# Single-value copies of VectorE moved ahead of the third block's statistics at the layer change of a two-layer graph network

## The chip, the core and the metric

The kernel runs on one core of a Trainium2 chip. Five engines work side by side, each through its own list of instructions in order: TensorE multiplies matrices (the profile shows it as PE, and its weight loads as PEld), VectorE (DVE), ScalarE (ACT) and GpSimd (POOL) do the element-wise work, and SyncE (SP) issues DMA transfers. Instructions of different engines meet only at semaphores: an instruction waits until a counter of another engine has reached a number. TensorE writes its results to PSUM[...], from which VectorE and ScalarE read.

The metric is the device time of one execution in microseconds, the median of three runs. All figures below in us are from such runs or from one profiled execution.

## The reference, cut to what matters

There are 8 batch elements `x[b]` of 2048 tokens and 256 features, and one adjacency matrix of 2048 x 2048. Layer 0 is an attention with four heads whose softmax runs over chunks of 256 keys, with output projection, residual and two normalisations. Layer 1 is a graph attention:

```python
h = relu(layernorm(x))                       # layer 1: statistics over the 256 features
h = h @ W                                    # 2048 x 256
e_src, e_dst = h @ a1, h @ a2                # one value per token each
e = where(adj == 0, -1e9, leaky_relu(e_src[:, None] + e_dst[None, :], 0.01))
x = x + relu(softmax(e) @ h)
```

The kernel keeps `W` with two further columns, `W a1` and `W a2`, in `w1s` (128 x 2 x 258), so that one matrix product gives `h` (256 columns) and the two values per token (columns 256 and 257) at once.

## The kernel before

**Tiling.** A batch element is cut into four blocks of 512 tokens, called `zero`, `low`, `mid` and `last` (class `Between`), and a block into four tiles of 128 tokens (`TB = 4`). Between the attention of one batch element and the products of its graph attention lies a stretch of some 45 us, the layer change, written out by hand from `if ahead:` on (line 1260). `ahead` is the projection of the next batch element: its matrix products are laced into the layer change of the present one. There are 8 batch elements; the first 7 take the branch `if ahead`, the last one the `else` branch, which the change does not touch.

**Order.** The kernel runs under a manual schedule: on every engine the instructions stand in the order in which the Python calls make them. A wait at the head of an engine's list therefore holds everything behind it on that engine.

**The steps that meet here**, in the order of the calls before the change:

- `mid.stats1([t])` (`Between.stats1`, which calls `norm_stats`, lines 356 and 357): `bn_stats` and `bn_aggr` of VectorE over tile `t` of the third block's `x4`. Tiles 2 and 3 of that block are finished by a GpSimd addition, `x<-x,o` at line 792 (`mid.add(1)`), which stands in GpSimd's list behind the issue of the last `ctxT<-prod` transfer (line 578, `gather`).
- `low.values(t, bank)` (line 843): two matrix products of 128 x 258 into a PSUM tile. Tiles 0 and 1 go to `ps_s` buffers, tiles 2 and 3 to `ps_t` buffers.
- `low.keep(t)`: ScalarE copies 256 columns to `g` (line 851), then VectorE copies the two last columns to `sd` (line 852, 128 x 2, two single values per token). Only when both are done can TensorE write to that PSUM buffer again.
- `low.sum1()` (line 838, ScalarE), `zero.fetch1()` (line 155, a DMA).
- `mid.power1()`, `mid.shift1()`, `mid.norm1(0)`, `mid.norm1(1)`: ScalarE (lines 361 to 363), VectorE (line 367, `rn`), ScalarE (line 379). They need the statistics of all four tiles.
- `ahead.values(0)` (line 461): eight matrix products of 128 x 256 into a `ps_n` buffer, then eight into a `ps_t` buffer; VectorE adds a bias and moves each to `v` (line 466).
- `ahead.qk(1, 0, halves=[0])` (line 447): four products of 128 x 512 into a `ps_n` buffer.
- `last.output(0)`, `last.output(1)` (line 721): eight products each from `ctxT`, which the transfer of line 578 completes; into a `ps_t` and a `ps_n` buffer. VectorE takes them up at line 757.

**PSUM.** The tags `s`, `n` and `t` have two buffers each. In this stretch `ps_m()` hands out `ps_n` and `ps_t` by turns. So the first `ps_t` of `ahead.values(0)` is the buffer that held `low.values(2)`, and the `ps_t` of `last.output(0)` the one that held `low.values(3)`. In the built program the first product of `ahead.values(0)` on `ps_t` waits for VectorE's count up to the copy of tile 2, and that of `last.output(0)` for the count up to the copy of tile 3.

**What waits for what on ScalarE.** In the built program each copy of line 852 waits for the ScalarE copy of line 851 of its own tile; both read the same PSUM buffer.

Of the kernel before, what the change touches and what calls it, by code (L numbers as in the profile page):

```python
# [28 lines left out]
def gnn_two_layers(  # L29
# [26 lines left out]
    TB = NB // P  # L56
# [335 lines left out]
    class Projection:  # L392
# [40 lines left out]
        def fetch(self, nb):  # L433
            self.hT[nb] = Features(turned_d[0][nb])
# [47 lines left out]
    class Attention:  # L482
# [100 lines left out]
        def early(self, part):  # L583

            if part == 0:
                for kt in range(KT):
                    self.logits(0, 0, kt)
                    self.logits(0, 1, kt)
            elif part == 1:
                for o in range(2):  # L590
                    self.clip(0, o)
                    self.exponentials(0, o)
                for kt in range(KT):
                    self.logits(0, 2, kt)
                    self.logits(0, 3, kt)
            elif part == 2:
                self.clip(0, 2)
                self.exponentials(0, 2)
                self.clip(0, 3)
                self.add(0, 0)  # L600
            if part == 3:
                for kt in range(KT):
                    self.logits(1, 0, kt)
# [305 lines left out]
    class Layer1:  # L909
# [56 lines left out]
        def weights(self, nb, j4, tiles=range(4), w=None):  # L966
            if w is None:
                w = work.tile([P, 4, NB], F32, tag="e", name="w", bufs=5)
            for i in tiles:
                j = 4 * j4 + i  # L970
                nc.vector.tensor_scalar(  # L971
                    w[:, i, :], self.src[nb], self.cd[:, 0, j:j + 1], self.cd[:, 1, j:j + 1],
                    op0=ALU.mult, op1=ALU.max,
                )
                if i % 2:
                    two = w[:, i - 1:i + 1, :]
                    nc.vector.scalar_tensor_tensor(  # L977
                        two, bounds1[nb, j // 8][:, j % 8 - 1:j % 8 + 1, :], 0.0, two, op0=ALU.is_gt, op1=ALU.mult
                    )
            return w  # L980
# [186 lines left out]
    for b in range(B):  # L1167
# [3 lines left out]
        zero, low, mid, last = blocks  # L1171
# [87 lines left out]
            block.adder = nc.vector  # L1259
        if ahead:  # L1260
            for t in range(TB):
                mid.stats1([t])
                low.values(t, ps_h if t < 2 else ps_t)
                low.keep(t)
            low.sum1()
            zero.fetch1()
            mid.power1()
            mid.shift1()
            mid.norm1(0)
            mid.norm1(1)  # L1270
            ahead.values(0)
            ahead.fetch(2)
            ahead.qk(1, 0, halves=[0])
            last.output(0)
            last.output(1)
            mid.flip1(0, "both")
            last.take(0)
            mid.flip1(1)
            last.take(1)
            mid.send1()  # L1280
            one.send(1)
            zero.sum1()
            last.stats(range(TB))
            ahead.qk(1, 0, halves=[1])
            last.power()
            last.shift()
            last.scaled(range(TB))
            ahead.qk(1, 1)
            for t2 in range(2):
                last.gamma(t2)  # L1290
                last.add(t2)
            for t in range(TB):
                last.stats1([t])
                zero.values(t)
                zero.keep(t)
            one.send(0)
            mid.fetch1()
            last.power1()
            last.shift1()
            last.norm1(0)  # L1300
            last.norm1(1)
            ahead.values(1)
            ahead.qk(2, 0)
            last.flip1(0, "both")
            last.flip1(1)
            last.send1()
            ahead.fetch(3)
            mid.sum1()
            ahead.qk(2, 1)
            mid.ends(1)  # L1310
            last.fetch1()
            one.receive(0)
            ahead.values(2)
            one.targets(0, 3 * TB)
            one.received(0)
            one.receive(1)
            ahead.qk(3, 0)
            weights(0)
            ahead.qk(3, 1)
            last.sum1()  # L1320
            last.ends(1)
            one.total()
            one.targets(3 * TB, NT)
            weights(1)
            one.send(2)
            one.send(3)
            ahead.values(3)
        else:
            one.weights(0, 0, range(2, 4), ws[0])
            low.ends(1, [ps_t, ps_t, ps_n, ps_n])  # L1330
            low.sum1()
            one.send(1)
            mid.stats1(range(TB))
            mid.power1()
            mid.shift1()
            accs[0] = one.accumulators(0)
            early(0)
            mid.norm1(0)
            mid.norm1(1)
            one.targets(TB, 2 * TB)  # L1340
            one.receive(1)
            last.output(0)
            last.output(1)
            weights(1)
            last.take(0)
            last.take(1)
            mid.ends(0)
            last.stats(range(TB))
            for t in range(TB):
                if t == 2:  # L1350
                    last.power()
                    last.shift()
                mid.values(t)
                mid.keep(t)
            one.targets(2 * TB, 3 * TB)
            weights(2)
            fetch(11)
            last.scaled(range(TB))
            one.received(1)
            for t2 in range(2):  # L1360
                last.gamma(t2)
                last.add(t2)
            early(1)
            last.stats1(range(TB))
            last.power1()
            last.shift1()
            weights(3)
            last.norm1(0)
            last.norm1(1)
            early(2)  # L1370
            last.ends(0)
            one.total()
            last.ends(1)
            one.mean()
            one.targets(3 * TB, NT)
            weights(4)
            fetch(12)
            one.send(2)
            one.send(3)
            one.receive(2)  # L1380
            one.alone(0)
# [81 lines left out]
```

## Time and profile before

| | us |
|---|---|
| median of 3 runs | 3513.77 |
| lowest and highest run | 3513.32, 3514.57 |
| profiled execution, its own time | 3513.01 |
| span of the profiled execution (first to last instruction) | 3511.2 |
| DVE busy | 2630.4 (75%) |
| ACT busy | 1959.2 (56%) |
| POOL busy | 1825.5 (52%) |
| mean granted TensorE clock | 1.000 |

The span is 1.8 us shorter than the time of the same execution; that rest lies before the first and after the last instruction of the program. The seven layer changes of the branch `if ahead` begin at 347.81, 781.25, 1214.26, 1647.28, 2080.35, 2513.36 and 2946.38 us (the first product of line 843 on `ps_s`), so a batch element takes about 433.0 us. The granted clock is full throughout, so no stretch has to be corrected for it.

In the rows of a timeline the first number is the start in us from the beginning of the span, the second the duration from the first start to the last end of the row's instructions, then follow engine, line, operation, `out<-in`, shapes and the number of instructions. In brackets stands how long the engine idled before the row and who ended that. A row of `x8` is eight instructions that follow each other.

### The profile page before, as it was taken

What the parts mean: (1) busy time and instruction counts of PE and PEld (TensorE: products, weight loads), DVE (VectorE), ACT (ScalarE), POOL (GpSimd) and SP (SyncE); (2) the same over time, 40 slices, a digit from 0 to 9 for tenths busy, and PEclk for the clock granted to TensorE, in tenths of its full rate; (3) what the DMA queues carried; (4) which work ended last, traced back from release to release, by engine and by line L of the source; (5) the groups of instructions that cost most, each with busy time, mean ns of one, the idle gap of its engine ahead of it and who ended that gap; (6) DMA issues with size and microseconds to landing.
All of it is one profiled execution on the core that took longest, in us unless ns stands there. A gap on an engine that the chain in (4) does not pass through costs nothing.

```text
span 3511.2 us, 104599 instructions
## 1 busy us (share of the span) xinstructions
PE 3498.5 (100%) x46076; PEld 2300.0 (66%) x46076; DVE 2630.4 (75%) x3983; ACT 1959.2 (56%) x2961; POOL 1825.5 (52%) x1198
## 2 busy tenths in 40 slices
PE   9999999999999999999999999999999999999999
PEld 5455775667765577566876758656686655864568
DVE  7887677877678676786767867678686785857876
ACT  6777426763267633676336763367623776147751
POOL 5687017870278702786037850378503784047841
PEclk9999999999999999999999999999999999999999
DMA  7545323443234431444324443244432335224331
GB/s 246 129 108 123 94 87 73 97 113 102 68 87 86 118 100 61 92 93 109 102 61 92 92 105 102 66 91 87 119 105 64 79 85 125 63 55 92 80 78 53
DMA packets 171320, 332.13 MB, mean 95 GB/s; under 512 B 28656, under 2 KB 90352, under 8 KB 170864
## 3 DMA queue, kind: packets, MB, share of 16 engines
q1 hardware_dynamic: 129712, 205.36, 18.6%
q0 software_dynamic: 32832, 119.03, 18.5%
q8 instruction: 360, 5.90, 0.7%
q10 hardware_dynamic: 8320, 1.05, 0.2%
q14 instruction: 96, 0.79, 0.1%
HBM read 156.50 MB, written 51.44 MB: 59 GB/s over the span
## 4 chain that ended last, share of the span: by engine, by line
PE 97%; DVE 1%; ACT 1%; POOL 1%; issue 0%; DMA 0%; ACTq 0%; DVEq 0%; POOLq 0%
PE ps_s L503 25%; PE ps_n L519 25%; PE ps_s L994 12%; PE ps_t L531 6%; PE ps_n L994 6%; PE ps_t L994 6%; PE ps_t L743 2%; PE ps_t L447 2%; PE ps_n L447 2%; PE ps_s L447 2%; PE ps_t L461 2%; PE ps_n L461 1%; PE ps_n L843 1%; PE ps_t L843 1%; PE ps_z L296 0%
## 5 line engine op out<-in xcount | busy, mean ns | idle before, releaser
L543 DVE SCALAR_TENSOR_TENSOR e<-ps_s,bound 128x1024 f32<-128x1024 f32 x1024 | 1219.3, 1221 | 401.3 <-PE ps_s L503 396.4
L558 POOL TENSOR_TENSOR both<-e 128x1024 f32<-128x1024 f32 x512 | 1222.4, 2418 | 541.8 <-PE ps_t L531 244.6
L503 PE MATMUL ps_s<-q,k 64*32 64x512 f32 x16384 | 1335.2, 590 | 0.1
L552 ACT ACTIVATE e<-e 128x1024 f32<-128x1024 f32 x1024 | 1049.3, 1049 | 456.2 <-DVE e L543 438.8
L519 PE MATMUL ps_n<-e,v 64*32 64x512 f32 x16384 | 1121.2, 589 | 0.0
L503 PEld LDWEIGHTS ps_s<-q,k 64*32 64x32 f32 x16384 | 505.2, 106 | 403.3 <-issue 277.9
L519 PEld LDWEIGHTS ps_n<-e,v 64*32 64x32 f32 x16384 | 522.0, 107 | 366.3 <-issue 266.5
L531 PE MATMUL ps_t<-both,ones 64*32 64x512 f32 x4096 | 548.7, 590 | 0.0
L994 PE MATMUL ps_s<-g,w 128*128 128x257 f32 x2048 | 448.5, 380 | 0.0
L994 PEld LDWEIGHTS ps_s<-g,w 128*128 128x128 f32 x2048 | 388.4, 190 | 56.0
L573 DVE TENSOR_TENSOR prod<-ps_n,rz 128x512 f32<-128x512 f32 x448 | 288.7, 687 | 135.0 <-ACT rz L564 86.5
L1017 POOL TENSOR_TENSOR x<-x,r 128x256 f32<-128x256 f32 x124 | 90.7, 745 | 457.8 <-ACT r L1015 457.0
L977 DVE SCALAR_TENSOR_TENSOR w<-bound,w 128x1024 f32<-128x1024 int8 x256 | 314.7, 1229 | 8.7
L367 POOL TENSOR_TENSOR krn<-krn,mv 128x4 f32<-128x4 f32 x28 | 6.8, 243 | 566.1 <-DVE w L971 566.1
L994 PE MATMUL ps_n<-g,w 128*128 128x257 f32 x1024 | 292.4, 382 | 0.0
L994 PE MATMUL ps_t<-g,w 128*128 128x257 f32 x1024 | 289.7, 380 | 0.0
L563 ACT ACTIVATE rz<-ps_t 128x512 f32<-128x512 f32 x256 | 152.6, 596 | 237.3 <-PE ps_t L531 164.2
L971 DVE TENSOR_SCALAR w<-src,cd 128x512 f32<-128x512 f32 x512 | 263.2, 556 | 18.1 <-ACT src L951 14.2
L994 PEld LDWEIGHTS ps_n<-g,w 128*128 128x128 f32 x1024 | 192.8, 190 | 44.3 <-issue 17.6
L578 POOL DMA_DIRECT2D ctxT<-prod x224 | 192.3, 858 | 56.5 <-DVE prod L573 49.5
L531 PEld LDWEIGHTS ps_t<-both,ones 64*32 64x32 f32 x4096 | 152.3, 105 | 100.7 <-SPq L475 45.1
L994 PEld LDWEIGHTS ps_t<-g,w 128*128 128x128 f32 x1024 | 193.8, 189 | 28.2
(139 smaller groups left out, 2975.2 us busy)
## 6 DMA issues: line engine op xcount, KB each, us to landing
ctxT<-prod POOLq DMA_DIRECT2D x224, 512.0 KB, 5.0
bound<-bound_d SPq DMA_DIRECT2D x125, 512.0 KB, 4.7
turned_d<-squares SPq DMA_DIRECT2D x232, 128.0 KB, 2.9
hT<-turned_d SPq DMA_DIRECT2D x58, 512.0 KB, 4.5
rows<-in_adj_dram SPq DMA_DIRECT2D x32, 512.0 KB, 5.3
x<-in_x_dram SPq DMA_DIRECT2D x32, 512.0 KB, 6.3
out_dram<-x SPq DMA_DIRECT2D x31, 512.0 KB, 2.6
xp<-in_x_dram SPq DMA_DIRECT2D x28, 512.0 KB, 4.4
```

Source lines behind the costliest of these rows:

```text
L447: nc.tensor.matmul(in_key_order(pp) if i == 0 else pp, w[:, di, do * P:(do + 1) * P], h, start=di == 0, stop=di == FC - 1,)
L503: nc.tensor.matmul(self.s[n, o][c * Q:(c + 1) * Q, kt, :], self.k[p][rows, at:at + Q], self.q[p][rows, nb * NB:(nb + 1) * NB], start=True, ...
L519: made.append(nc.tensor.matmul(self.num[n, c][h * Q:(h + 1) * Q, :], self.v[rows, j * KT + kt, at:at + Q], self.e[n, p][rows, i * KT + kt, :],
L531: nc.tensor.matmul(self.total[n][h * Q:(h + 1) * Q, :], ones[rows, :], self.both[n, h // 2][rows, h % 2, :], start=half == 1, stop=half == 0,)
L543: nc.vector.scalar_tensor_tensor(self.e[n, p][:, i * KT:(i + 1) * KT, :], self.s.pop((n, o)), -CLIP * SC, bounds[nb, j // 4][:, j % 4 * KT ...
L552: nc.scalar.activation(e, e, AF.Exp, scale=1.0 / SC)
L558: nc.gpsimd.tensor_tensor(self.both[n, p], e[:, 0], e[:, 1], op=ALU.add)
L573: nc.vector.tensor_tensor(dst[:, c, :], self.num.pop((n, c)), self.rz[n], op=ALU.mult)
L578: nc.gpsimd.dma_start(self.ctxT[nb], self.prod.pop(n), accum_op=ALU.add)
L971: nc.vector.tensor_scalar(w[:, i, :], self.src[nb], self.cd[:, 0, j:j + 1], self.cd[:, 1, j:j + 1], op0=ALU.mult, op1=ALU.max,)
L977: nc.vector.scalar_tensor_tensor(two, bounds1[nb, j // 8][:, j % 8 - 1:j % 8 + 1, :], 0.0, two, op0=ALU.is_gt, op1=ALU.mult)
L994: nc.tensor.matmul(accs[t][:, 0:F + 1], w[:, i, t * P:(t + 1) * P], g[:, j, :], start=j == 0, stop=j == NT - 1,)
```

## The change

In the first lines of the branch `if ahead` the order of the calls is altered. Nothing is added or removed; the number of instructions on each engine is the same.

```diff
         if ahead:
             for t in range(TB):
-                mid.stats1([t])
                 low.values(t, ps_h if t < 2 else ps_t)
                 low.keep(t)
+                if t:
+                    mid.stats1([t - 1])
+            mid.stats1([TB - 1])
             low.sum1()
```

`low.values` issues only to TensorE and `low.keep` to ScalarE and VectorE, `mid.stats1` only to VectorE. So the lists of TensorE, ScalarE, GpSimd and SyncE stay as they are, instruction for instruction. VectorE's list changes in seven places, one in each layer change with a next batch element:

```
before: stats 0, copy 0, stats 1, copy 1, stats 2, copy 2, stats 3, copy 3
after:  copy 0, copy 1, stats 0, copy 2, stats 1, copy 3, stats 2, stats 3
```

Here "stats t" stands for the two instructions of lines 356 and 357, and "copy t" for the one of line 852. In the built program the waits follow: the `ps_t` product of `ahead.values(0)` waits for a VectorE count that is lower by four (copy 2 stands two tiles' statistics nearer the front), the first product of `last.output(0)` again for the count of copy 3, and ScalarE's line 361 for the count of the last aggregation in place of that of copy 3.

## The prediction, made before the changed kernel ran

> **What bounds the kernel now.** I read the page's first and fourth parts first: which engine is never idle, and which one the end hangs on.
>
> ```profile
> PE 3498.5 (100%) x46076; PEld 2300.0 (66%) x46076; DVE 2630.4 (75%) x3983; ACT 1959.2 (56%) x2961; POOL 1825.5 (52%) x1198
> PE 97%; DVE 1%; ACT 1%; POOL 1%; issue 0%; DMA 0%; ACTq 0%; DVEq 0%; POOLq 0%
> ```
>
> TensorE is idle for 3511.2 - 3498.5 = 12.7 us and carries 97% of the chain of waits. What the other engines do counts only where it makes TensorE wait, so the second view is the list of who waited for the copies of line 852:
>
> ```profile
>   PEld ps_t L461: 7.1, 7
>   PE ps_t L461: 4.3, 7
> ```
>
> TensorE stood still seven times in front of the second half of `ahead.values(0)`, until a copy of two values per partition was done: one stall for each layer change that has a next batch element. The third view is the timeline there, TensorE first, in the third of the seven:
>
> ```profile
> 1216.11 1.91 PE L843 MATMUL ps_t<-w1s,hT 128*128 128x258 f32 x8
> 1217.86 1.89 PE L461 MATMUL ps_n<-wvT,hT 128*128 128x256 f32 x8
> 1220.30 1.99 PE L461 MATMUL ps_t<-wvT,hT 128*128 128x256 f32 x8 [0.55 <-DVE sd L852]
> 1222.13 1.88 PE L447 MATMUL ps_n<-hT,wqT 128*128 128x512 f32 x4
> 1223.85 1.89 PE L721 MATMUL ps_t<-woT,ctxT 128*128 128x256 f32 x8
> 1225.57 1.89 PE L721 MATMUL ps_n<-woT,ctxT 128*128 128x256 f32 x8
> ```
>
> Then VectorE, and the GpSimd rows that it waits for:
>
> ```profile
> 1217.52 0.13 DVE L852 COPY sd<-ps_s 128x2 f32<-128x2 f32 x1
> 1217.57 0.42 DVE L356 BATCH_NORM_STATS2 stats<-x 128x6 f32<-128x256 f32 x1
> ...
> 1219.55 0.43 DVE L356 BATCH_NORM_STATS2 stats<-x 128x6 f32<-128x256 f32 x1 [1.31 <-POOL x L792]
> 1220.02 0.18 DVE L357 BATCH_NORM_AGGREGATE mv<-stats 128x2 f32<-128x6 f32 x1
> 1220.12 0.13 DVE L852 COPY sd<-ps_t 128x2 f32<-128x2 f32 x1
> ```
>
> ```profile
> 1217.35 0.86 POOL L578 DMA_DIRECT2D ctxT<-prod  x1 [7.19 <-DVE prod L573]
> 1217.96 1.56 POOL L792 TENSOR_TENSOR x<-x,o 128x512 f32<-128x512 f32 x1
> ```
>
> The copy of tile 2 is not late by itself: it stands behind the statistics of tile 2, and these wait 1.31 us for GpSimd's addition, which ends at 1219.52. A short copy is held by a wait that it does not need, and TensorE is held by the copy (done 1220.25, product at 1220.30).
>
> **What the stall costs.** The page's idle time is measured against modelled ends, so I take starts. Eight products of 128x256 occupy 1225.57 - 1223.85 = 1.72 us when nothing is in the way; from the `ps_n` half to the `ps_t` half it is 1220.30 - 1217.86 = 2.44, 0.72 too much. The stalled half itself takes 1222.13 - 1220.30 = 1.83, another 0.10 too much (its row is 1.99 long against 1.89): the pipe has to fill again. Together 0.82 us. In the first layer change the halves start at 351.41 and 354.27 and the next row at 356.10: 2.86 - 1.73 + 0.10 = 1.23, since GpSimd's issue of the transfer, and so its addition, comes 0.42 later there (start 3.52 us after the first product of line 843, against 3.09). The other five are like the third: of the 4.3 us in the list above 0.97 is the first one's, and 6 x 0.55 = 3.3 the rest; VectorE's waits for that addition, 9.6 us in seven times, are in the same way 1.73 + 6 x 1.31. Sum: 1.23 + 6 x 0.82 = **6.15 us**.
>
> Rule against row: the Trainium skill, "Perfetto Trace Analysis", section "Identifying the Most-Contended Engine", says that busy time of the matmuls is no good measure of how near TensorE is to its limit, because they are pipelined, and that the busy share of the weight loads is to be used. For this sum the matmul rows would give 4.3 us of idle time, the weight loads 7.1. The starts decide between them: 4.3 leaves out the tail that the model adds to the last product, 7.1 takes in a pause that a weight load has before an undisturbed product too. 4.3 and 7.1 are the two ends that I keep for the range.
>
> **The change part by part.**
>
> *Copies 0 and 1 in front of statistics 0.* Two instructions of 0.13 to 0.16 us. Their ScalarE copies ended at 1216.01 and 1216.70, before VectorE is through with `prod` (1217.06), so they start at once. They delay statistics 0 and 1 by about 0.1 us each; nobody reads these before statistics 3 is done. Cost 0; the cover is VectorE's idle 1.31 us.
>
> *Copy 2 in front of statistics 1.* Two copies, one pair of statistics and the copy after 1217.06: 0.06 + 0.06 + 0.42 + 0.14 + 0.13, so done by about 1217.8, where the undisturbed `ps_t` half is due at 1217.86 + 1.72 = 1219.58. Margin 1.8 us: the stall goes whole. The rows of VectorE overlap (the copy at 1217.52 runs to 1217.65, the statistics start at 1217.57), so a copy holds the next operation up by some 0.05; at its full 0.16 it would be 1218.0, and the margin would hold too.
>
> *Copy 3 in front of statistics 2.* It has to wait for ScalarE's copy of tile 3. "PSUM — Partial Sum Buffer", section "PSUM bank collisions raise a hardware error", asks that two engines be kept apart on one bank even where both read, and the program does have VectorE wait for ScalarE. The rule speaks against putting such copies ahead of work that needs no ScalarE. The row:
>
> ```profile
> 1218.05 0.38 ACT L851 ACTIVATE g<-ps_t 128x256 f32<-128x256 f32 x1 [0.49 <-PE ps_t L843]
> ```
>
> It ends at 1218.43. VectorE reaches copy 3 at about 1218.3, waits 0.15 and is done at 1218.6, still 0.9 us before GpSimd frees statistics 2. By the rule up to 0.2 us of VectorE's time, by the rows none on the path: 0.
>
> *Statistics 2 and 3 without copies between them.* The last aggregation ends at about 1220.75, where copy 3 ended at 1220.84. ScalarE's line 361 waits for that, so `power1`, `shift1` and `norm1` come 0.08 earlier. Nothing for TensorE.
>
> **What is late next.** TensorE reaches line 447 at 1221.3 and `last.output(0)` at 1223.03 (first layer change: 356.58). That needs `ctxT`: issued at 1217.35, landed 4.7 us later by the DMA view of this window, 1222.1 (first: 351.33 + 4.8 = 356.1). Margins 0.9 and 0.4: no new wait. `last.output(1)`, due at 1224.75, needs the `ps_n` buffer that line 466 empties; VectorE is through with that at 1222.5, behind line 367. Margin 2.2. All that follows (line 757, the last block's statistics, the transfers of its and `mid`'s turned tiles) hangs on these products and moves up with them. From 1260 to 1647 the view of stretches shows TensorE busy for all of 140.00 and 247.00 us, so there is no later wait that could eat the gain. A second small hole, 7 x 0.17 us before `ahead.values(1)` (line 461 on `ps_n`, 2.2 us of the weight loads' waits for line 852), is at the end of such a chain and stays as it is.
>
> **Sum.** The profiled execution took 3513.01; minus 6.15 gives 3506.9. The median of the runs shown is 0.76 higher, so I forecast **3507.6**. A difference of less than 0.2%, 7.03 us, can't be told from no change here; the forecast lies inside it by 0.9 us.
>
> **The rivals.**
> - *More than the stall goes* (0.13). If the 7.1 us of the weight loads are the truer measure, or the small second hole closes too (6.15 + 1.2 = 7.35), the time is 3506.4 to 3506.7, faster by just over the bound. For: both numbers stand in the profile. Against: the chain into the second hole moves up with TensorE, so the hole should stay.
> - *The transfer takes the stall's place* (0.08). The margin before `last.output(0)` is 0.4 to 0.9 us, and over the whole program this transfer lands after 4.5 to 7.8 us. Landing 1.3 us later than now would give back 0.4 to 0.9 in each, some 3 us: 3510.6; more than 1.8 us later gives back all: 3513.8. Against: the transfer's issue and its neighbours are unchanged, and in the two layer changes that I read it took 4.7 and 4.8.
> - *The stall doesn't go* (0.04): another wait sits under the same product. Then 3513.8. The built order lists only VectorE's count there.
> - *ScalarE holds the copies, and these the statistics* (0.05): the slower side. Copy 3 now stands ahead of statistics 2 and 3 and waits for ScalarE. If it came later than 1219.5, the whole row statistics, lines 361 to 367, line 466 would be late. Its end must leave 3.0 us for that row before 1224.75, so it decides from about 1221.7 on; to cost 7 us beyond the gain, (6.15 + 7.0)/7 = 1.9 us more each, ScalarE's copy would have to end at 1223.6 and not at 1218.43. Time 3520.8. Its list is unchanged, hence the small chance.
>
> **How the numbers follow.** The forecast has 0.70: 3506.8 to 3508.4 with the spread of the runs (1.25 us from lowest to highest). The range, 3506.3 to 3510.6, takes in the first rival and half of the second. Faster by over 0.2%: 0.13 and the lower tail of the forecast, together 0.20. Slower: 0.06. Within: 0.74.
>
> **What would show it.** Right: the waits for line 852 no longer name `PE ps_t L461`; its `ps_t` half starts 1.72 us after its `ps_n` half; the sixteen products' rows are both 1.89 long; VectorE's idle time before statistics 2 is still ended by GpSimd; from one layer change to the next it is 432.2 us, not 433.0. Wrong: a new idle time in brackets before line 721 or 843, above all one ended by a DMA or by ScalarE, or an unchanged 433.0.

## The result, and the profile after

| | before | after |
|---|---|---|
| median of 22 runs, us | 3513.81 | 3507.69 |
| span of the profiled execution, us | 3511.2 | 3506.3 |
| start of the first layer change, us | 347.81 | 349.03 |
| from one layer change to the next, us | 433.44, then 433.01 to 433.07 | 432.19 to 432.27 |

The change saves 6.12 us: the ratio is 0.9983, with an interval from 0.9977 to 0.9989, that is 3.9 to 8.1 us. The saving is 0.17%, inside the 0.2% within which the forecast counted a difference as none, and yet clear of no change with this many runs. Three single runs far above the rest (20027.53 us before, 8030.45 and 4592.26 after) are not in the ratio; without them the medians are 3513.80 and 3507.67. The spans differ by 4.9 only because the set-up of this one execution, before the first layer change, took 1.2 us longer; counted from there to the end, 3163.4 us became 3157.3, 6.1 less.

The first part of the page, and from the view of who waited for the copies of line 852 the group of those that waited:

```profile
PE 3496.3 (100%) x46076; PEld 2309.8 (66%) x46076; DVE 2630.3 (75%) x3983; ACT 1958.5 (56%) x2961; POOL 1824.3 (52%) x1198
```

```profile
who waited for it (us, times):
  POOL ctxT L578: 50.2, 7
  ACT rn L361: 8.7, 8
  ACT cd L933: 3.6, 16
  PEld ps_n L461: 2.2, 7
  PEld ps_s L843: 0.2, 1
```

The two rows for `ps_t L461`, 4.3 and 7.1 us, are gone; `ps_n L461` with 2.2 is still there. (That GpSimd's `ctxT` stands in the list is no new wait: the transfer goes out 3.09 us into the layer change as before. The view names the last count of VectorE before that, now a copy's.) TensorE's timeline in the third layer change, which begins at 1213.42:

```profile
1217.01 1.89 PE L461 MATMUL ps_n<-wvT,hT 128*128 128x256 f32 x8
1218.73 1.89 PE L461 MATMUL ps_t<-wvT,hT 128*128 128x256 f32 x8
1220.46 1.88 PE L447 MATMUL ps_n<-hT,wqT 128*128 128x512 f32 x4
1222.18 1.89 PE L721 MATMUL ps_t<-woT,ctxT 128*128 128x256 f32 x8
```

Each row starts 1.72 or 1.73 us after the one above, no idle time stands in brackets, and both rows of line 461 are 1.89 long: neither the stall nor the filling of the pipe is left. VectorE beside it:

```profile
1216.12 0.22 DVE L852 COPY sd<-ps_s 128x2 f32<-128x2 f32 x2
...
1216.81 0.13 DVE L852 COPY sd<-ps_t 128x2 f32<-128x2 f32 x1
...
1217.62 0.16 DVE L852 COPY sd<-ps_t 128x2 f32<-128x2 f32 x1
1218.70 0.43 DVE L356 BATCH_NORM_STATS2 stats<-x 128x6 f32<-128x256 f32 x1 [0.92 <-POOL x L792]
```

Statistics 2 still wait for GpSimd's addition, and start at the same moment as before, 5.28 us into the layer change (5.29 before); only no copy stands behind them any more.

### The profile page after: what moved, and what is told of

Same layout as the page of the kernel before. It is cut to its first block, busy times and chain, and to the rows that moved or that the text cites. A ratio compares the mean times of both kernels' runs of the same rounds, so it can differ in the third digit from the quotient of the medians.

```text
span 3506.3 us, 104599 instructions
## 1 busy us (share of the span) xinstructions
PE 3496.3 (100%) x46076; PEld 2309.8 (66%) x46076; DVE 2630.3 (75%) x3983; ACT 1958.5 (56%) x2961; POOL 1824.3 (52%) x1198
## 4 chain that ended last, share of the span: by engine, by line
PE 98%; DVE 1%; DMA 1%; ACT 0%; POOL 0%; issue 0%; ACTq 0%; DVEq 0%; POOLq 0%
PE ps_s L503 25%; PE ps_n L519 25%; PE ps_s L994 12%; PE ps_t L531 6%; PE ps_n L994 6%; PE ps_t L994 6%; PE ps_t L743 2%; PE ps_t L447 2%; PE ps_n L447 2%; PE ps_s L447 2%; PE ps_n L461 2%; PE ps_t L843 1%; PE ps_t L461 1%; PE ps_n L843 1%; PE ps_s L843 0%; DMA bound_d<-bound_part 0%
```

## The experiments

All times are medians of 6 to 21 runs, to be held against 3513.8 to 3514.0 for the kernel before in the same sessions and 3507.69 for the changed one. The 95% interval of each ratio is 0.0013 to 0.0025 wide, 5 us and more, so differences of some 1 us are read from the profiled execution instead: from the start of the first layer change to the end, where the kernel before takes 3163.4 us and the changed one 3157.3.

### Which copy carries the gain

Of the kernel before, copy 2 alone is moved, ahead of statistics 2:

```diff
-                mid.stats1([t])
+                if t != 2:
+                    mid.stats1([t])
                 low.values(t, ps_h if t < 2 else ps_t)
                 low.keep(t)
+                if t == 2:
+                    mid.stats1([t])
```

> The kernel before with one copy moved: VectorE's copy of tile 2 ahead of statistics 2, copies 0, 1 and 3 where they were. My theory (copy 2 alone holds TensorE, by standing behind statistics 2 that wait for GpSimd): the whole gain, 6.15 us, 3507.7, and the ps_t half of line 461 starts 1.72 us after the ps_n half. Rival (all the copies in front, or the shorter row of statistics, bring the gain): at most a part of it, 3510 or more.

Measured: 3507.64 us, ratio 0.9982 (0.9974 to 0.9989). One exchanged pair brings the whole gain (3157.3 us from the first layer change to the end, as in the changed kernel). The counterpart has copies 0 and 1 in front and leaves 2 and 3 behind their statistics:

```diff
-                mid.stats1([t])
+                if t == 2:
+                    for u in range(3):
+                        mid.stats1([u])
+                if t == 3:
+                    mid.stats1([t])
```

> The kernel before with copies 0 and 1 in front, but copy 2 behind statistics 2 and copy 3 behind statistics 3 as before. My theory: no gain, 3513.8, and the stall of 0.72 us before the ps_t half stays, 0.97 idle in the first layer change and 0.55 in the others. Rival (any relief of VectorE's list ahead of the statistics helps): a part of the 6.15 us, 3508 to 3512.

Measured: 3513.81 us, ratio 1.0 (0.9992 to 1.0008). TensorE's timeline there (its third layer change begins at 1215.01):

```profile
1218.60 1.89 PE L461 MATMUL ps_n<-wvT,hT 128*128 128x256 f32 x8
1221.04 1.99 PE L461 MATMUL ps_t<-wvT,hT 128*128 128x256 f32 x8 [0.55 <-DVE sd L852]
```

It is the stall of before to the hundredth: 2.44 from start to start, 0.55 idle, and from the first layer change to the end it takes 3163.4 us as before. Two of the four copies moved without any effect.

### Is it the copy's place, or GpSimd's lateness

VectorE's list as before; GpSimd's addition goes half an attention step earlier:

```diff
-            at(18 if soon else 20, lambda: self.add(1))
+            at(18 if soon else 19 if self.nb == NNB - 2 else 20, lambda: self.add(1))
```

> The kernel before, VectorE's list untouched; GpSimd's addition (line 792, second half of the third block) is issued half an attention step earlier, ahead of the last ctxT transfer in GpSimd's list. My theory: statistics 2 no longer wait, copy 2 is done about 1.0 us before TensorE wants the buffer, and the whole 6.15 us are gained without moving a copy: 3507.7. Rival (VectorE's own work ahead of copy 2, eight instructions, is what is too long): the stall shrinks only in part, 3510 to 3513.

Measured: 3508.12 us, ratio 0.9984 (0.9977 to 0.9991). VectorE's timeline, third layer change from 1214.64:

```profile
1218.54 0.42 DVE L356 BATCH_NORM_STATS2 stats<-x 128x6 f32<-128x256 f32 x1
1219.00 0.18 DVE L357 BATCH_NORM_AGGREGATE mv<-stats 128x2 f32<-128x6 f32 x1
1219.10 0.13 DVE L852 COPY sd<-ps_t 128x2 f32<-128x2 f32 x1
```

With the addition done in time the statistics do not wait, and copy 2, still behind three pairs of them, is done at 1219.23, when TensorE wants the buffer only at 1214.64 + 5.32 = 1219.96. So the stall needs both: a copy behind the statistics, and statistics that wait for GpSimd. To remove either is enough. The 0.4 us that this version stays behind is visible in the trace (3157.8 against 3157.3): line 757 now waits for GpSimd too, which takes one more semaphore instruction, so it starts 12.48 and not 12.41 us into the layer change, and the products behind the second hole start 0.07 later, seven times.

### What the slower side would have taken

All four copies in front, so that VectorE waits for ScalarE with none of the statistics done:

```diff
-                mid.stats1([t])
                 low.values(t, ps_h if t < 2 else ps_t)
                 low.keep(t)
+            for t in range(TB):
+                mid.stats1([t])
```

> All four copies ahead of all four statistics. VectorE then waits for ScalarE's copy of tile 3 (ends 4.17 us after the first product of line 843) with nothing done of the statistics; the last aggregation ends some 0.2 us later than in the changed kernel (6.6 against 6.46). My theory: that is inside the margin, 3507.7. Rival (a wait for ScalarE put in front of the statistics is passed on to TensorE): 0.2 us in each of seven layer changes, 3509.1, or more if the normalisation is late for line 466.

Measured: 3508.00 us, ratio 0.9983 (0.9976 to 0.999). The two expectations lie 1.4 us apart and the runs of one kernel spread by more (3507.24 to 3509.85), so the time alone leans to the first without deciding. TensorE's starts decide for the first: they are those of the changed kernel to 0.01 us in the whole third layer change. To find where the margin ends, work for nobody is put between statistics 2 and 3 of the changed kernel:

```diff
+            spare = small.tile([P, TB, 2], F32, tag="spare", name="spare", bufs=2)
+            norm_stats(mid.x4, spare, [0] * 3)      # 8 in the second kernel
             mid.stats1([TB - 1])
```

> The changed kernel with three more pairs of statistics (tile 0 again, into a tile that nobody reads) on VectorE between statistics 2 and 3: some 3 x 0.53 = 1.6 us more before lines 361, 367, 379 and 466. My theory (the row of statistics has a margin of 2.2 us before it empties the ps_n buffer that the second half of line 721 needs): no loss, 3507.7, at most 3508.5 where the two transposes come close to line 757. Rival (work on VectorE in this stretch is passed on to TensorE): 7 x 1.6 = 11 us, 3519.

> The same with eight more pairs, some 4.2 us. My theory: the margin is used up, the second half of line 721 starts about 2.0 us late, 0.1 for filling the pipe again, and up to 0.5 more at the next hole, line 461 of the second block: 7 x 2.6 = 18 us, 3526. Rival (passed on in full): 7 x 4.2 = 30, 3537. Rival (all hidden): 3507.7.

Measured: 3507.37 and 3524.39 us, ratios 0.9981 (0.9973 to 0.999) and 1.003 (1.0018 to 1.0042). 1.6 us of additional work seven times cost nothing; 4.2 us cost (3524.39 - 3507.69)/7 = 2.4 each, so what is passed on begins between the two. Where it comes out, from the list of TensorE's waits and its timeline (third layer change from 1217.31), both with eight more pairs:

```profile
PE ps_n L721 <- DVE v L466: 12.3, 7, 2.1
```

```profile
1226.07 1.89 PE L721 MATMUL ps_t<-woT,ctxT 128*128 128x256 f32 x8
1229.65 1.99 PE L721 MATMUL ps_n<-woT,ctxT 128*128 128x256 f32 x8 [1.69 <-DVE v L466]
```

It is the place that the prediction named, the `ps_n` buffer of line 466. The second half starts 3.58 us after the first instead of 1.72, 1.86 late; with the pipe to fill and the next holes a little wider that makes the 2.4. 2.6 was expected. Line 466 starts 3.95 us later than in the changed kernel and 1.86 of this is passed on, so its margin is 2.1 us, where the prediction had 2.2.

### The second hole

The same exchange where the statistics of the last block and the copies of the first block's values alternate:

```diff
-                last.stats1([t])
                 zero.values(t)
                 zero.keep(t)
+                if t:
+                    last.stats1([t - 1])
+            last.stats1([TB - 1])
```

> The changed kernel, and the same reordering at the second such place, where the statistics of the last block and the copies of the first block's values alternate. There TensorE stands 0.07 us and fills its pipe for 0.10 before line 461 on ps_n, seven times 0.17. My theory: the copies have nothing to wait for, so the hole closes: 1.2 us, 3506.5. Rival (the hole is of another cause, or moves to the next product): 3507.7.

Measured: 3506.44 us, ratio to before 0.9979 (0.997 to 0.9988). The two timelines, first the changed kernel, then this one:

```profile
1233.40 1.03 PE L843 MATMUL ps_t<-w1s,hT 128*128 128x258 f32 x4
1234.35 1.99 PE L461 MATMUL ps_n<-wvT,hT 128*128 128x256 f32 x8
```

```profile
1232.51 1.03 PE L843 MATMUL ps_t<-w1s,hT 128*128 128x258 f32 x4
1233.38 1.89 PE L461 MATMUL ps_n<-wvT,hT 128*128 128x256 f32 x8
```

0.95 from start to start has become 0.87, and the row is 0.10 shorter: 0.18 x 7 = 1.26 us, and 3507.69 - 3506.44 = 1.25 are measured (1.3 in the trace, 3156.0 against 3157.3). This version is faster than both kernels.

### The transfer's margin

The prediction gave line 721 a margin of 0.4 to 0.9 us over the landing of `ctxT`. To use it up, the issue is held back in GpSimd's list until copy 3 is done (GpSimd's addition of line 792, no longer behind it, is then over before the layer change begins):

```diff
+            after_copies = small.tile([P, 1], F32, tag="held", name="held", bufs=2)
+            nc.gpsimd.tensor_copy(after_copies, sd[:, 0, 2 * TB - 1:2 * TB])
+            att.gather(STEPS - 1)       # no longer issued within the attention
             zero.fetch1()
```

> The changed kernel, the issue of the last ctxT transfer held in GpSimd's list until VectorE's copy 3 is done (a one-element copy of GpSimd in front of it waits for that): issued some 1.5 us later, at about 4.6 us after the first product of line 843, landing at about 9.4, where line 721 is due at 8.76. My theory of the transfer's margin (0.9 us, 0.4 in the first layer change): line 721 stands 0.6 to 0.75 us and fills its pipe for 0.1, the gain is about given back, 3512.5 to 3513.5. Rival (ample cover, or line 721 waits for something later than the transfer already): 3507.7.

Measured: 3525.20 us, ratio 1.0033 (1.002 to 1.0045). Both expectations failed: 17.5 us were lost and not 5 to 6. From the list of TensorE's waits, from its timeline and from the DMA view of the third layer change (there the last figure is from issue to landing), the late transfer; line 723 is line 721 of the other kernels:

```profile
PE ps_t L723 <- DMA ctxT<-prod: 14.5, 7, 3.6
```

```profile
1230.95 1.97 PE L723 MATMUL ps_t<-woT,ctxT 128*128 128x256 f32 x8 [1.79 <-DMA ctxT<-prod]
```

```profile
hT<-turned_d SPq DMA_DIRECT2D x2, 512.0 KB, 5.9
ctxT<-prod POOLq DMA_DIRECT2D x1, 512.0 KB, 5.9
```

The issue came at 4.67 us, as meant, but the transfer took 5.9 us and not 4.7, and in the first layer change 7.3. The changed kernel's, in the same view:

```profile
ctxT<-prod POOLq DMA_DIRECT2D x1, 512.0 KB, 4.7
```

In flight beside it from 5.42 and 7.24 us on are two loads of 512 KB (line 155). Two more kernels tell whether these did it: the same late transfer with both loads held on SyncE until `mid`'s first half is turned, and as a control the changed kernel with the loads held and the transfer in its usual place.

```diff
-            zero.fetch1()                # and ahead.fetch(2)
 ...
             mid.flip1(0, "both")
+            after_flip = nc.vector.tensor_copy(held2[:, 1:2], held2[:, 0:1])
+            tc.add_manual_dep(nc.sync.nop().ins, after_flip.ins.name, SYNC, reason="hold the loads")
+            zero.fetch1()
+            ahead.fetch(2)
```

> As the run before with the ctxT transfer issued at 4.67 us, but the two loads of turned features (line 155) that were in flight beside it are held on SyncE until VectorE has turned mid's first half (about 8.6 us). Theory A (in the run before, the transfer took 5.9 us and not 4.75 because those loads ran beside it): it lands at about 9.4 to 9.6 again, line 721 stands 0.7 to 0.8 us and fills its pipe for 0.1; 7 x 0.85 and some 0.5 more in the first layer change: 3514 to 3515. Theory B (the transfer is slow by itself when issued there): landing at 10.6, 3524 to 3525.

> Control: the changed kernel with the same two loads held until mid's first half is turned (about 9.7 us here), the transfer issued as usual at 3.09. The held loads land at about 14 to 15 us and are wanted at 17.4 and 20.8. Both theories: no loss, 3507.7; under theory A the transfer lands no later than 7.8, perhaps a little earlier than in the changed kernel (4.75 us after its issue). A loss here, above 3509, would say that holding the loads costs time by itself and has to be taken off the run with the late transfer.

Measured: 3512.74 us, ratio 0.9997 (0.9989 to 1.0006), and 3507.82 us, ratio 0.9983 (0.9976 to 0.9989). The late transfer without company, in the DMA view and in TensorE's timeline:

```profile
ctxT<-prod POOLq DMA_DIRECT2D x1, 512.0 KB, 4.5
```

```profile
1223.64 1.97 PE L723 MATMUL ps_t<-woT,ctxT 128*128 128x256 f32 x8 [0.36 <-DMA ctxT<-prod]
```

The same transfer, issued at the same moment, takes 4.5 us instead of 5.9 when the loads are away, and TensorE's idle time before it falls from 1.79 us to 0.36. Holding the loads by itself costs next to nothing (the control: 3157.5 us from the first layer change to the end against 3157.3). So of the 17.5 us lost, 5.1 (3512.74 - 3507.69) belong to the later issue and 12.5 (3525.20 - 3512.74) to the two loads that ran beside it.

Some 1.8 of these 12.5 us came by a way that no expectation had. In the first layer change of the profiled execution TensorE stood for 3.60 us, and then its granted clock fell to one half. First its timeline, then the view of stretches from 362.00 to 365.40 us, where the third figure from the right is the clock:

```profile
360.83 2.65 PE L723 MATMUL ps_t<-woT,ctxT 128*128 128x256 f32 x8 [3.60 <-DMA ctxT<-prod]
```

```profile
362.00:365.40 3.40, 3.40 (x9) 2.66 (x8) 1.31 (x2) 0.00 (x0) 0.00 (x0) 0.50 0.00 0
```

The two halves of line 723 take 2.44 and 2.77 us there from start to start instead of 1.72 and 1.73. In the other six layer changes of this run, after 1.78 to 1.87 us of idle time, the clock stayed full, as it did in all seven with the loads held. (The mean clock reads 0.999 in each of the six runs of this kernel, so it will have fallen in all of them.)

The kernel with the late transfer alone ended below its expectation of 3514 because in four of the seven layer changes the transfer took 4.5 us, less than the 4.75 that I had carried over from a transfer with company. In the other three it took 4.8 to 5.0; what made it longer there is not shown.

## Why the prediction was right

*The size of the stall* was right: 6.15 us forecast from starts, 6.12 measured. That the medians agree so closely is luck, since their interval, 3.9 to 8.1 us, would also hold the other two readings, 4.3 from TensorE's idle rows and 7.1 from its weight loads. The starts decide: 1.25 us were saved in the first layer change and 0.80 to 0.83 in each of the other six, against 1.23 and 0.82, together 6.15.

*Why the weight loads gave 7.1* was read wrongly, as a pause that they have before an undisturbed product too. There is none. In the changed kernel the sixteen loads follow each other without idle time, each half beginning some 0.2 us ahead of its products (those of this row start at 1218.73):

```profile
1218.52 1.70 PEld L461 LDWEIGHTS ps_t<-wvT,hT 128*128 128x128 f32 x8
```

In the kernel before, the stalled half's loads and products both start at 1220.30. The loads' idle time of 0.95 us is thus the stall of 0.72 and this lost lead of 0.2.

*The cause* was right and is now shown by taking each half away: copy 2 alone brings all (3507.64), copies 0 and 1 nothing (3513.81), the addition in time does the same as the moved copy (3508.12).

*The moved copies cost nothing*: they start at 1216.12, copy 2 is done at 1216.94, 3.52 us into the layer change, with TensorE due at 5.32: margin 1.8 as said. (The five terms of the prediction's sum end at 1217.87, not 1217.8; measured, copy 2 is done 0.73 us after `prod` where they make 0.81. The sum left out that copy 2 waits for ScalarE as well; ScalarE's copy of tile 2 ended at 1216.73, before VectorE came to it at 1216.81.) Copy 3 does wait for ScalarE: it starts at 1217.62, 0.13 us after VectorE is free and just after ScalarE's copy of tile 3 ends at 1217.59. The program keeps the two engines apart on one bank, as the Trainium skill, "PSUM — Partial Sum Buffer", section "PSUM bank collisions raise a hardware error", asks even where both only read. Copy 3 ends 0.9 us before GpSimd frees the statistics, so the wait costs nothing.

*"`power1`, `shift1` and `norm1` come 0.08 earlier"* holds for the first only. Line 361 starts 6.49 instead of 6.57 us into the layer change, but VectorE's line 367 ends at 7.72 in both kernels, because it takes 0.42 us in place of 0.35 (see the last section). Nothing on TensorE depended on it.

*The margins behind the stall* were right: the transfer lands at 7.81, 0.95 before line 721 (8.38 in the first layer change, 0.38 before); the row of statistics can be 1.6 us later for nothing and is felt at line 466 when it is 4.2 later.

*The rivals.* The second hole stays as long as nothing is done about it; it needs its own exchange, and then brings the 1.2 us that were named. The price of a later landing was about right: "landing 1.3 us later" was to give back 0.4 us in a layer change, and with the late transfer alone it gave back 0.47 to 0.51 in the four where it landed 1.3 later. Wrong was to take the duration as fixed, in the expectation for the late transfer: beside the loads a delay of the issue by 1.6 us moved the landing by 2.8. The chance of that rival was not affected, since the change leaves the issue where it was.

## What to carry to other kernels

Where an engine is 100% busy on the page, look for who waited for it in single places and measure the hole from start to start; the idle time and the weight loads gave 4.3 and 7.1 us for a hole of 6.1. On an engine that works strictly in order, put the short instruction that frees another engine's buffer ahead of long ones that wait for a third engine, and look only for the one that is waited for: one of four moved copies did the work. Before moving the issue of a transfer, see what else will be in flight then: here the company cost more than the delay.

## What the runs showed of the hardware

- The transfer of 512 KB `ctxT<-prod` by GpSimd's queue took 4.5 us with both loads issued after it had landed (4.5 to 5.0 where it was issued late and they followed near its end), 4.7 to 4.8 with a load of 512 KB issued 2.3 us after it, and 5.9 to 6.0 with one issued 0.75 us after it. A second load, issued at 7.24 us, ran beside the late transfer too; what each of the two costs is not shown.
- After TensorE had stood for 3.60 us, the granted clock was 0.50 for 3.4 us, beginning 1.2 us after its first product, and a product of 128 x 256 took 0.63 us instead of 0.38. In the layer changes this was seen once, in the first one with the late transfer beside the loads; after idle times of up to 1.87 us in the same run, and up to 2.1 us with eight more pairs of statistics, it did not come. How long TensorE must stand for it is not shown.
- After a wait of TensorE at full clock the first row of eight products was 0.08 to 0.10 us longer (1.97 to 1.99 against 1.89). With the model's tail a stall costs more than its idle time: 0.82 us for the 0.55 of the kernel before.
- VectorE's line 367, 128 x 4 elements from two tiles in SBUF, ends 0.03 us after GpSimd's addition of line 788 wherever the two overlap: in all seven layer changes of each of eight kernels, before and after among them, with 0.35 to 0.84 us for the row. GpSimd's row in the changed kernel ends at 1221.10, VectorE's at 1221.13:

```profile
1218.34 2.76 POOL L788 TENSOR_TENSOR x<-x,beta_r 128x512 f32<-128x512 f32 x2
```

```profile
1220.71 0.42 DVE L367 TENSOR_TENSOR rn<-rn,mv 128x4 f32<-128x4 f32 x1 [0.84 <-ACT rn L363]
```

With three more pairs of statistics it starts after GpSimd is done, and takes 0.16:

```profile
1221.25 0.16 DVE L367 TENSOR_TENSOR rn<-rn,mv 128x4 f32<-128x4 f32 x1 [0.84 <-ACT rn L363]
```

Whether other instructions of VectorE with two inputs are held in the same way is not shown.
- In the first layer change the transfer's issue comes 0.42 us later than in the other six, in every kernel, also where it was held back (5.10 against 4.67). Why is open.
